# Six shared PSUM banks in an attention-then-Mamba kernel: gates into the convolutions' banks, reciprocals turned in the denominators' bank, and attention steps at fixed half slots

## The chip, the core and the metric

The kernel runs on one core of a Trainium2 chip. The metric is the device time of one execution in microseconds (us). Five engines work side by side: TensorE (PE; its weight loads are shown as PEld), VectorE (DVE), ScalarE (ACT), GpSimd (POOL), and SyncE (SP), which only issues DMA transfers here. Each engine takes its own instructions in the order in which the program put them.

## The reference, cut to what matters

```python
# x: (8, 512, 48, 48) float32; L = 48*48 = 2304 tokens
# layer 0: x = x + attention(group_norm(x)), 8 heads of 64, causal linear attention
Q = elu(q) + 1;  K = elu(k) + 1
den = 1 / (Q . cumsum(K) + 1e-10)
out = (causal sum of K V^T, applied to Q) * den
# layer 1: x = x + mamba_stack(group_norm(x)); 4 blocks of 128 channels, one after the other
xz = u @ Wi.T;  xp, z = split(xz)
xs = silu(causal_conv4(xp) + bc)                    # 256 inner channels
dt, Bm, Cm = split(xs @ Wx.T);  delta = softplus(dt @ Wdt.T + bdt)
h_t = exp(delta A) h_(t-1) + delta xs Bm            # 16 states per channel
y = (sum over states of h C + xs D) * silu(z);  xm = y @ Wo.T
feat = sigmoid(mean x_i) x_i + sigmoid(mean max(x_i, xm)) max(x_i, xm)   # passed to the next block
```

## The kernel before, in words

**Mamba: jobs and slots.** Two streams handle the even and the odd samples. Each of the 8 x 4 blocks (sample, channel block) is cut into six pieces of 384 tokens (`LC`), so there are 192 **jobs**. A job has 8 **slots**; a slot is four scans on VectorE (`Job.scan`, L830, 128 x 385), one product ahead of them (`product`, L809) and a weighing on GpSimd (`weigh`, L846). 1,536 slots follow one another. The decay of every scan, exp(delta A), is computed by ScalarE (`decay`, L819) into a PSUM bank; the k-th decay belongs to the k-th scan, and the bank is free again once that scan has read it. `ahead(n)` issues decays until n are waiting, as long as a bank is spare: three are asked for after each scan, five ahead of the two groups that change ScalarE's table of functions, which are the Silu group (L670 to L675) and the Softplus group (L705).

**Banks.** Six PSUM banks (`BANKS`) are shared by the decays and by everything else that TensorE writes, except the sum over states, which has its own (`yp`, L853). `take` gives out the first spare bank; banks that are freed `late`, that is after a Silu or Softplus group, are kept back for decays where another is spare.

**Halves.** Each slot has two **halves**: one ahead of its four scans, one after the second of them. In a half, `beside` lets the tasks step that are due and for which enough banks are spare; a task is a Python generator whose `yield` says when it may go on (a number of halves after its last step, or a fixed half) and how many banks it needs. So the Python decides the order, and each engine then works its own queue.

**A job's preparation** (`prepare`) runs about ten slots ahead of its scans: two convolutions with the input projection folded in (`conv`, L635, four accumulating matmuls each), two gate projections (`gate`, L646), the Silu group (`xs` twice, `sz` twice), the projection to dt, B, C (L681, copied out at L686), the step projection (L694), Softplus, then writes to DRAM and the repeated reads of `dr`, `dxr`, B and C. A job that is done ends in `finale`: the output projection (L871) one half after the last product with the gate (`gated`, L865), and the maximum on VectorE (`fg`, L882) one half later.

**Attention: chunks.** 192 **chunks** (sample, head pair o, 384 tokens) run beside the jobs, most of them 16 halves apart (`PERIOD`), in step with the jobs. A chunk's steps stand at fixed halves after its start, `at(j)`: projections q, k, v (L288), feature maps (exp and relu on ScalarE at L300 and L301, then L345 for q and L353 for k on VectorE), key sums (L364, L374), turned k and v (L381), denominators and state increments (L393, L398; read at L401 to L410), the reciprocals copied wide (L414) and turned (L418), q times the reciprocals (L423), scores (L431, L436), outputs (L445, L449, L452). A group norm ahead of either layer needs the statistics of a sample (`statistics`, L242) or of one block (`group_norm` at L457).

With the two period lengths equal, a chunk starts at half 3 of a job's 16 halves, and a job's preparation falls on fixed halves as well.

Of the kernel before, what the change touches and what calls it, by code (L numbers as in the profile page):

```python
# [9 lines left out]
F32 = mybir.dt.float32  # L10
# [6 lines left out]
P = 128  # L17
T = 128
LC = 384
# [30 lines left out]
def attention_then_mamba_kernel(  # L50
# [108 lines left out]
            _, o, i = stores.pop(0)  # L159
            nc.sync.dma_start(out=o, in_=i)  # L160

    def group_norm(stats, n, name, bufs):


        bank = Banks()
        yield "1", 1
        mv = small.tile([P, n, 2], F32, tag=f"mv{n}", name=f"mv_{name}", bufs=1)
        for ct in range(n):
            nc.vector.bn_aggr(mv[:, ct, :], stats[:, ct].rearrange("p c s -> p (c s)"))
        mean_ps = bank()  # L170
        nc.tensor.matmul(mean_ps[:, 0:n], grp, mv[:, :, 0], start=True, stop=True)
        yield "1", 0
        gm = small.tile([P, 3, n], F32, tag=f"gm{n}", name=f"gm_{name}", bufs=1)
        nc.vector.tensor_copy(gm[:, 0, :], mean_ps[:, 0:n])
        nc.vector.tensor_sub(gm[:, 1, :], mv[:, :, 0], mean_ps[:, 0:n])
        bank.free()
        if n == 1:
            nc.vector.tensor_scalar(
                gm[:, 2, :], gm[:, 1, :], gm[:, 1, :], mv[:, 0, 1:2], ALU.mult, ALU.add
            )  # L180
        else:
            nc.vector.tensor_mul(gm[:, 2, :], gm[:, 1, :], gm[:, 1, :])
            nc.vector.tensor_add(gm[:, 2, :], gm[:, 2, :], mv[:, :, 1])
        yield "0", 1
        var_ps = bank()
        nc.tensor.matmul(var_ps[:, 0:n], grp, gm[:, 2, :], start=True, stop=True)
        yield "1", 0
        nc.vector.tensor_scalar_add(gm[:, 2, :], var_ps[:, 0:n], 1e-5)
        bank.free()
        norm = small.tile([P, 3, n], F32, tag=f"norm{n}", name=f"norm_{name}", bufs=bufs)  # L190
        nc.gpsimd.tensor_tensor(norm[:, 0, :], gm[:, 2, :], power[:, 0:n], ALU.pow)
        yield "1", 0
        for i, factor in ((0, -1.0), (1, float(L))):
            for ct in range(n):
                nc.vector.tensor_scalar(
                    norm[:, 1 + i, ct : ct + 1],
                    gm[:, i, ct : ct + 1],
                    norm[:, 0, ct : ct + 1],
                    factor,
                    ALU.mult,  # L200
                    ALU.mult,
                )
        return norm
# [5 lines left out]
    def statistics(b):  # L209

        xv = x[b].rearrange("(t p) l -> p t l", p=P)
        stats = small.tile([P, 4, NC, 6], F32, tag="stats_a", name=f"stats_a{b}", bufs=1)
        if b == 0:

            xs = []

            def load(c):
                t = mpool.tile([P, 4, 1 + LC], F32, tag="u", name=f"xs_{c}", bufs=5)[:, :, 0:LC]
                nc.sync.dma_start(out=t, in_=xv[:, :, c * LC : (c + 1) * LC])
                xs.append(t)  # L220

            for c in range(5):
                load(c)
            load_projections(0)
            for c in range(NC):
                for ct in range(4):
                    nc.vector.bn_stats(stats[:, ct, c, :], xs[c][:, ct, :])
                if c == 0:
                    load(5)
                    fetch(0)  # L230
            for o in range(1, 4):
                load_projections(o)
        else:
            for ct in range(4):
                for c in range(NC):
                    yield "2", 0
                    if (ct, c) == (0, 0):
                        nxt = piece(b, 0)
                    xs = nxt
                    i = ct * NC + c + 1  # L240
                    nxt = piece(b, i) if i < 4 * NC else None
                    nc.vector.bn_stats(stats[:, ct, c, :], xs)  # L242
        norms[b] = yield from group_norm(stats, 4, f"a{b}", 2)

    def piece(b, i):
        ct, c = i // NC, i % NC
        xs = apool.tile([P, LC], F32, tag="xs", name=f"xs_{b}_{i}", bufs=2)
        nc.sync.dma_start(out=xs, in_=x[b][ct * P : (ct + 1) * P, c * LC : (c + 1) * LC])
        return xs
# [18 lines left out]
    def chunk(m):  # L268
# [71 lines left out]
        qp, qb = project(0)  # L340
        yield at(1), 0
        ex = feature(qp, qb)
        yield at(2), 0
        q = new("q", 2)
        nc.vector.scalar_tensor_tensor(q, ex, 1.0, qp, ALU.min, ALU.add)  # L345
        bank.free()
        yield at(2, 0), 1
        kp, kb = project(1)
        yield at(3), 0
        ex = feature(kp, kb)  # L350
        yield at(4), 0
        k = new("k", 2)
        nc.vector.scalar_tensor_tensor(k, ex, 1.0, kp, ALU.min, ALU.add)  # L353
        bank.free()
        yield at(4, 0), 1
# [10 lines left out]
            nc.tensor.matmul(kc, ident, before, start=False, stop=True)  # L366
        yield at(8), 0
        if ksum is not None:
            kept = new("kept")
# [16 lines left out]
        nc.scalar.copy(v, turned[1])  # L386
        bank.free(2)

        yield at(12), 1
        both = bank()  # L390
        den = both[:, 0 : 2 * NT]
        for i in range(NT):
# [3 lines left out]
        for i in range(more):  # L396
            for h in heads_of:
                nc.tensor.matmul(ds[h, i, :], kl[:, i, h], v[:, i, h], start=True, stop=True)  # L398
        yield at(14), 0
        rd = small.tile([P, 2 * NT], F32, tag="rd", name=f"rd_{n}", bufs=1)  # L400
        nc.vector.tensor_scalar_add(rd, den, 1e-10)  # L401
        nc.vector.reciprocal(rd, rd)
# [3 lines left out]
        for i in range(more):  # L406
            if c == 0 and i == 0:
                nc.vector.tensor_copy(S[:, place[1], :], ds[:, 0, :])
            else:
                nc.vector.tensor_add(S[:, place[i + 1], :], S[:, place[i], :], ds[:, i, :])  # L410
        bank.free()
        yield at(15), 0
        rdb = new("rdb", 1, (P, 2 * NT, 64))
        nc.scalar.copy(rdb, rd.unsqueeze(2).to_broadcast([P, 2 * NT, 64]))  # L414
        yield at(16), 1
        rb = bank()[:, 0:LC].rearrange("p (i t) -> p i t", i=NT)
        for i in range(NT):
            nc.tensor.transpose(  # L418
                rb[:, i, :], rdb[:, 2 * i : 2 * i + 2, :].rearrange("p e d -> p (e d)"), ident
            )  # L420
        yield at(18), 0

        nc.vector.tensor_mul(q, q, rb.rearrange("p i t -> p (i t)"))  # L423
        bank.free()
# [29 lines left out]
        nc.vector.bn_stats(stats[:, 0, c, :], xr)  # L454
        save(x1s[b][tile_rows, cols], xr)
        if c + 1 == NC:
            norm = yield from group_norm(stats, 1, f"m{b}_{o}", 8)  # L457
            flush()
            done[b, o] = norm

# [155 lines left out]
    class Job:  # L616
# [6 lines left out]
        def prepare(self):  # L623
# [17 lines left out]
                    )  # L641
                return xc

            def gate(h):
                zp = bank()[:, 0:LC]
                nc.tensor.matmul(  # L646
                    zp,
                    wi[:, 256 + h * P : 256 + (h + 1) * P],
                    xi[:, c0 + 3 : c0 + 3 + LC],
                    start=True,  # L650
                    stop=True,
                )
                return zp


            while converting or not st.scaled:
                yield "1w", 0
            converting.append(n)
            yield "1", 1
            xc0 = conv(0)  # L660
            yield "2", 2
            xc1 = conv(1)
            zp0 = gate(0)
            yield "1", 0
# [5 lines left out]
            nc.scalar.activation(xs[:, 0, :], xc0, AF.Silu, bias=pv[:, 0:1])  # L670
            bank.free()
            zp1 = gate(1)
            nc.scalar.activation(xs[:, 1, :], xc1, AF.Silu, bias=pv[:, 1:2])
            nc.scalar.activation(sz[0], zp0, AF.Silu)
            nc.scalar.activation(sz[1], zp1, AF.Silu)  # L675
            converting.clear()
            bank.free(3, late=True)
            yield "1", 1
            dps = bank()
            for h in range(2):  # L680
# [54 lines left out]
            def rows(m, q):  # L735
# [5 lines left out]
                    )  # L741
                (self.B, self.C)[m][q] = t

            for h in range(2):
                yield "1", 0
                nc.gpsimd.tensor_tensor(delta[:, h, :], delta[:, h, :], xs[:, h, :], ALU.mult)  # L746
            first = 2 * self.start
            yield "2", 0
            xsrc = spread("xscr")
            spreading.clear()  # L750
# [206 lines left out]
    def finale(job):  # L957
# [4 lines left out]
        if job.c == NC - 1:  # L962
            yield from job.stream.pass_on()

    begun, put, counted = 0, 0, list(range(1, B))

    def begin(latest):

        nonlocal begun, put
        while counted and times[parts.index((counted[0], 0, 0))] - 64 <= half_no[0]:  # L970
# [53 lines left out]
    def at(k):  # L1024
        return jobs[k // SLOTS], k % SLOTS
# [166 lines left out]
```

## Time and profile before

| | before |
|---|---|
| median of 3 runs | 9331.63 us (9327.02 to 9333.99) |
| profiled execution | 9323.3 us, span 9321.5 us |
| busy: VectorE | 8348.4 us (90% of the span) |
| busy: GpSimd | 8080.8 us (87%) |
| busy: TensorE | 7735.1 us (83%) |
| busy: ScalarE | 6580.2 us (71%) |
| moved by DMA | 1642.84 MB, mean 176 GB/s |
| first 100 us: VectorE, GpSimd busy | 42.10 us, 20.79 us |

How to read what follows: a row of a timeline is start (us), duration (us), engine, line and operation, then out<-in with its sizes and how many instructions were merged. Brackets at its end give how long the engine had stood idle before it and what ended that. A row of the waits is: engine, line and tile that waited, `<-` whom it waited for, total us, times, longest us. One job takes about 48 us (9321.5 / 192 = 48.5).

### The profile page before, as it was taken

What the parts mean: (1) busy time and instruction counts of PE and PEld (TensorE: products, weight loads), DVE (VectorE), ACT (ScalarE), POOL (GpSimd) and SP (SyncE); (2) the same over time, 40 slices, a digit from 0 to 9 for tenths busy, and PEclk for the clock granted to TensorE, in tenths of its full rate; (3) what the DMA queues carried; (4) which work ended last, traced back from release to release, by engine and by line L of the source; (5) the groups of instructions that cost most, each with busy time, mean ns of one, the idle gap of its engine ahead of it and who ended that gap; (6) DMA issues with size and microseconds to landing.
All of it is one profiled execution on the core that took longest, in us unless ns stands there. A gap on an engine that the chain in (4) does not pass through costs nothing.

```text
span 9321.5 us, 120629 instructions
## 1 busy us (share of the span) xinstructions
PE 7735.1 (83%) x35714; PEld 3673.0 (39%) x35714; DVE 8348.4 (90%) x11640; ACT 6580.2 (71%) x12656; POOL 8080.8 (87%) x5635
## 2 busy tenths in 40 slices
PE   7888888888888888888888888888888888888865
PEld 4444444433344444443343444443333434444321
DVE  3899999999999999999999999999999999999997
ACT  3677777777777777777777777776777777777775
POOL 2788888889988898889998888888998888888998
PEclk9999999999999999999999999999999999999977
DMA  6566666667666666666766666667666666666654
GB/s 189 158 169 173 175 174 168 180 189 198 188 169 176 177 179 172 176 183 189 196 182 178 174 175 173 174 170 194 192 184 182 176 176 172 173 171 175 167 153 129
DMA packets 1002899, 1642.84 MB, mean 176 GB/s; under 512 B 138592, under 2 KB 797312, under 8 KB 1002240
## 3 DMA queue, kind: packets, MB, share of 16 engines
q1 hardware_dynamic: 1002240, 1635.13, 64.1%
q8 instruction: 283, 4.64, 0.2%
q14 instruction: 376, 3.08, 0.1%
HBM read 1309.06 MB, written 325.58 MB: 175 GB/s over the span
## 4 chain that ended last, share of the span: by engine, by line
DVE 39%; ACT 20%; PE 18%; issue 7%; DMA 7%; POOL 6%; SPq 2%; DVEq 0%; POOLq 0%; ACTq 0%
DVE u L830 23%; DVE u L809 8%; PE bank L288 7%; ACT bank L819 6%; PE bank L635 4%; POOL u L846 4%; ACT L819 3%; PE yp L853 3%; PE bank L646 2%; ACT L705 2%; DMA B<-scr 2%; DMA C<-scr 1%; ACT bank L301 1%; ACT delta L705 1%; DVE sm L436 1%
## 5 line engine op out<-in xcount | busy, mean ns | idle before, releaser
L830 DVE TENSOR_TENSOR_SCAN u<-bank,u 128x385 f32<-128x385 f32 (+1 forms) x6144 | 5475.1, 938 | 530.5 <-ACT bank L819 503.2
L846 POOL TENSOR_TENSOR u<-u,C 128x1536 f32<-128x1536 f32 x1536 | 4885.1, 3180 | 219.5 <-DVE u L830 112.6
L819 ACT ACTIVATE bank<-dr,av 128x385 f32<-128x385 f32 (+1 forms) x6144 | 3431.3, 579 | 1556.9 <-DVE u L830 1113.3
L853 PE MATMUL yp<-u,cst 128*64 128x384 f32 x12288 | 2429.9, 514 | 282.7 <-ACT yp L787 146.3
L798 POOL TENSOR_TENSOR u<-B,dxr 128x512 f32<-128x512 f32 x1536 | 1959.9, 1276 | 22.4 <-DMA dxr<-xscr 19.0
L288 PE MATMUL bank<-xn,wq_sb 128*128 128x384 f32 x4608 | 1855.1, 552 | 48.8 <-DVE u L830 31.7
L809 DVE TENSOR_TENSOR u<-B,dxp 128x1024 f32<-128x1024 f32 x1536 | 1834.7, 1195 | 10.7 <-ACT dxp L782 10.7
L853 PEld LDWEIGHTS yp<-u,cst 128*64 128x64 f32 x12288 | 788.3, 139 | 1476.6 <-issue 903.5
L635 PE MATMUL bank<-xi,wk 128*128 128x384 f32 x3072 | 1118.2, 507 | 280.1 <-ACT kl L385 172.7
L288 PEld LDWEIGHTS bank<-xn,wq_sb 128*128 128x128 f32 x4608 | 929.1, 212 | 862.9 <-issue 215.1
L635 PEld LDWEIGHTS bank<-xi,wk 128*128 128x128 f32 x3072 | 563.7, 193 | 862.2 <-ACT kl L385 254.1
L844 POOL COPY state<-u 128x4 f32<-128x4 f32 x1280 | 243.8, 190 | 740.6 <-DVE u L830 738.0
L300 ACT ACTIVATE ex<-bank,bqkv_sb 128x384 f32<-128x384 f32 x384 | 221.3, 576 | 561.6 <-PE bank L288 539.2
L787 ACT ACTIVATE yp<-xs,pv 128x384 f32<-128x384 f32 x384 | 223.4, 582 | 405.7 <-DVE yz L865 405.7
L819 ACT ACT_TABLE_LOAD x382 | 490.1, 1283 | 6.7
L746 POOL TENSOR_TENSOR delta<-delta,xs 128x384 f32<-128x384 f32 x384 | 385.8, 1005 | 95.5 <-DMA dscr<-delta 84.3
L418 PE MATMUL bank<-cst,rdb 128*128 128x128 f32 x576 | 112.7, 310 | 426.1 <-DVE u L830 334.7
L694 PE MATMUL bank<-dbc,wd 9*128 9x384 f32 x768 | 316.3, 524 | 65.1 <-ACT dbc L686 29.0
L646 PE MATMUL bank<-xi,wi 128*128 128x384 f32 x768 | 297.8, 500 | 59.8 <-ACT xs L670 59.8
L871 PE MATMUL bank<-yz,wo 128*128 128x384 f32 x768 | 297.6, 509 | 34.1 <-DVE yz L865 19.4
L449 PE MATMUL bank<-sm,v 128*64 128x128 f32 x2304 | 257.2, 301 | 42.4 <-DVE u L830 40.6
L418 PEld LDWEIGHTS bank<-cst,rdb 128*128 128x128 f32 x576 | 66.8, 153 | 558.9 <-ACT xb L601 272.5
(109 smaller groups left out, 7860.3 us busy)
## 6 DMA issues: line engine op xcount, KB each, us to landing
B<-scr SPq DMA_DIRECT2D x1536, 192.0 KB
C<-scr SPq DMA_DIRECT2D x1536, 192.0 KB
xn<-xn SPq DMA_DIRECT2D x192, 768.0 KB
dr<-dscr SPq DMA_DIRECT2D x768, 192.0 KB
dxr<-xscr SPq DMA_DIRECT2D x768, 192.0 KB
dscr<-delta SPq DMA_DIRECT2D x192, 384.0 KB
xscr<-delta SPq DMA_DIRECT2D x192, 384.0 KB
xn<-in_x SPq DMA_DIRECT2D x48, 768.0 KB
```

The lines of the kernel that those rows point to most:

```text
L288: nc.tensor.matmul(ps, wq_sb[:, kt, j * 512 + o * P : j * 512 + (o + 1) * P], xn[:, kt, :], start=(kt == 0), stop=(kt == 3),)
L635: nc.tensor.matmul(xc, wk[:, k, h * P : (h + 1) * P], xi[:, c0 + k : c0 + k + LC], start=(k == 0), stop=(k == 3),)
L646: nc.tensor.matmul(zp, wi[:, 256 + h * P : 256 + (h + 1) * P], xi[:, c0 + 3 : c0 + 3 + LC], start=True, stop=True,)
L694: nc.tensor.matmul(vp, wd[32:41, h * P : (h + 1) * P], dbc[32:41, :], start=True, stop=True)
L746: nc.gpsimd.tensor_tensor(delta[:, h, :], delta[:, h, :], xs[:, h, :], ALU.mult)
L798: nc.gpsimd.tensor_tensor(u[:, :, :, 1 + LC - TAIL :], self.B[s % 4][:, :, cols].unsqueeze(2).to_broadcast(shape), self.dxr[s // 4][:, :, ...
L809: nc.vector.tensor_mul(u[:, :, :, 1 : 1 + LC - TAIL], self.B[s % 4][:, :, cols].unsqueeze(2).to_broadcast(shape), self.dxp.unsqueeze(1).to ...
L819: nc.scalar.activation(dA[:, cols], self.dr[h][:, g, cols], AF.Exp, scale=self.w[6][:, 2 * h + g, q + j : q + j + 1],)
L830: nc.vector.tensor_tensor_scan(u[:, j, g, cols], dA[:, cols], u[:, j, g, cols], 0.0, ALU.mult, ALU.add,)
L846: nc.gpsimd.tensor_tensor(h, h, self.C[s % 4].unsqueeze(2).to_broadcast([P, NG, 2, LC]), ALU.mult)
L853: nc.tensor.matmul(self.yp[g * 64 : g * 64 + 64, 0:LC], pair_sum, u[:, j, g, 1:], start=False, stop=(s % 4 == 3 and j == NG - 1), skip_gro ...
L871: nc.tensor.matmul(self.xm[:, 0:LC], self.w[2][:, h, :], self.yz[:, h, :], start=(h == 0), stop=(h == 1),)
```

## The change

1. **Gates.** `gate` gets a bank passed in. Each gate projection is written into the bank of the convolution that has just been read by Silu, so the Silu group uses two banks instead of three or four. The convolutions, the second of which needed two spare banks, and the group now stand at fixed halves (20, 18 and 17 halves ahead of the job's first scan) instead of at the earliest half that fits.
2. **Reciprocals.** The chunk's bank of denominators and state increments (`both`) isn't freed after L410; the reciprocals are turned into that bank. Denominators start at `at(11)` (were 12), their reading at 13 (14), the wide copy at 14 (15), the turning at 15 (16), q times the reciprocals at 16 (18).
3. **q and k.** k's projection comes at `at(2)` ahead of q's step on VectorE (L345), which goes to `at(3)`; before, q's step came first and its bank was freed.
4. **Statistics.** A later sample's 24 `bn_stats` come one per 16 halves (two halves after their load) instead of one every two halves; the group norm of a block stands at fixed halves.
5. **Small things.** Both products delta*xs stand in one half; `kept` uses the buffer tag `before`; `stats_a` has two buffers.

The diff, cut:

```diff
-    def group_norm(stats, n, name, bufs):
+    def group_norm(stats, n, name, bufs, places=("1", "1", "0", "1", "1")):
...
-            for ct in range(4):
-                for c in range(NC):
-                    yield "2", 0
-                    if (ct, c) == (0, 0):
-                        nxt = piece(b, 0)
-                    xs = nxt
-                    i = ct * NC + c + 1
-                    nxt = piece(b, i) if i < 4 * NC else None
-                    nc.vector.bn_stats(stats[:, ct, c, :], xs)
+            when = begins[b] + b % 2
+            for i in range(4 * NC):
+                yield (when - 2, 1) if b > 1 else "1", 0
+                xs = piece(b, i)
+                yield (when, 1) if b > 1 else "1", 0
+                nc.vector.bn_stats(stats[:, i // NC, i % NC, :], xs)
+                when += PERIOD
...
-        yield at(2), 0
-        q = new("q", 2)
+        yield at(2), 1
+        kp, kb = project(1)
+        yield at(3), 0
+        q, k = new("q", 2), new("k", 2)
         nc.vector.scalar_tensor_tensor(q, ex, 1.0, qp, ALU.min, ALU.add)
         bank.free()
-        yield at(2, 0), 1
-        kp, kb = project(1)
-        yield at(3), 0
         ex = feature(kp, kb)
...
-        yield at(12), 1
+        yield at(11), 1
         both = bank()
...
-        yield at(14), 0
+        yield at(13), 0
         rd = small.tile([P, 2 * NT], F32, tag="rd", name=f"rd_{n}", bufs=1)
...
-        bank.free()
-        yield at(15), 0
+        yield at(14), 0
         rdb = new("rdb", 1, (P, 2 * NT, 64))
         nc.scalar.copy(rdb, rd.unsqueeze(2).to_broadcast([P, 2 * NT, 64]))
-        yield at(16), 1
-        rb = bank()[:, 0:LC].rearrange("p (i t) -> p i t", i=NT)
+        yield at(15), 0
+
+        rb = both[:, 0:LC].rearrange("p (i t) -> p i t", i=NT)
...
-        yield at(18), 0
+        yield at(16), 0
         nc.vector.tensor_mul(q, q, rb.rearrange("p i t -> p (i t)"))
         bank.free()
...
-            norm = yield from group_norm(stats, 1, f"m{b}_{o}", 8)
+            norm = yield from group_norm(
+                stats, 1, f"m{b}_{o}", 8, [(times[m] + j, 1) for j in (26, 27, 29, 30, 31)]
+            )
...
-            yield "1", 1
+            first = 2 * self.start
+            yield (first - 20, 1), 1
             xc0 = conv(0)
-            yield "2", 2
+            yield (first - 18, 2), 1
             xc1 = conv(1)
-            zp0 = gate(0)
-            yield "1", 0
+            yield (first - 17, 1), 0
...
             nc.scalar.activation(xs[:, 0, :], xc0, AF.Silu, bias=pv[:, 0:1])
-            bank.free()
-            zp1 = gate(1)
+
+            gate(0, xc0)
             nc.scalar.activation(xs[:, 1, :], xc1, AF.Silu, bias=pv[:, 1:2])
-            nc.scalar.activation(sz[0], zp0, AF.Silu)
-            nc.scalar.activation(sz[1], zp1, AF.Silu)
+            gate(1, xc1)
+            nc.scalar.activation(sz[0], xc0, AF.Silu)
+            nc.scalar.activation(sz[1], xc1, AF.Silu)
             converting.clear()
-            bank.free(3, late=True)
+            bank.free(2, late=True)
```

More of the change, by code (lines that the diff above doesn't have):

```diff
@@ L160, in flush @@
             nc.sync.dma_start(out=o, in_=i)
-    def group_norm(stats, n, name, bufs):
+    def group_norm(stats, n, name, bufs, places=("1", "1", "0", "1", "1")):
         bank = Banks()
-        yield "1", 1
+        yield places[0], 1
         mv = small.tile([P, n, 2], F32, tag=f"mv{n}", name=f"mv_{name}", bufs=1)
@@ L171, in group_norm @@
         nc.tensor.matmul(mean_ps[:, 0:n], grp, mv[:, :, 0], start=True, stop=True)
-        yield "1", 0
+        yield places[1], 0
         gm = small.tile([P, 3, n], F32, tag=f"gm{n}", name=f"gm_{name}", bufs=1)
@@ L183, in group_norm @@
             nc.vector.tensor_add(gm[:, 2, :], gm[:, 2, :], mv[:, :, 1])
-        yield "0", 1
+        yield places[2], 1
         var_ps = bank()
         nc.tensor.matmul(var_ps[:, 0:n], grp, gm[:, 2, :], start=True, stop=True)
-        yield "1", 0
+        yield places[3], 0
         nc.vector.tensor_scalar_add(gm[:, 2, :], var_ps[:, 0:n], 1e-5)
@@ L191, in group_norm @@
         nc.gpsimd.tensor_tensor(norm[:, 0, :], gm[:, 2, :], power[:, 0:n], ALU.pow)
-        yield "1", 0
+        yield places[4], 0
         for i, factor in ((0, -1.0), (1, float(L))):
@@ L211, in statistics @@
         xv = x[b].rearrange("(t p) l -> p t l", p=P)
-        stats = small.tile([P, 4, NC, 6], F32, tag="stats_a", name=f"stats_a{b}", bufs=1)
+        stats = small.tile([P, 4, NC, 6], F32, tag="stats_a", name=f"stats_a{b}", bufs=2)
         if b == 0:
@@ L342, in chunk @@
         ex = feature(qp, qb)
-        yield at(2), 0
-        q = new("q", 2)
+        yield at(2), 1
+        kp, kb = project(1)
+        yield at(3), 0
+        q, k = new("q", 2), new("k", 2)
         nc.vector.scalar_tensor_tensor(q, ex, 1.0, qp, ALU.min, ALU.add)
         bank.free()
-        yield at(2, 0), 1
-        kp, kb = project(1)
-        yield at(3), 0
         ex = feature(kp, kb)
         yield at(4), 0
-        k = new("k", 2)
         nc.vector.scalar_tensor_tensor(k, ex, 1.0, kp, ALU.min, ALU.add)
@@ L368, in chunk @@
         if ksum is not None:
-            kept = new("kept")
+            kept = new("before")
             nc.scalar.copy(kept[64:128], kc[64:128])
@@ L642, in conv, with gate @@
                 return xc
-            def gate(h):
-                zp = bank()[:, 0:LC]
+            def gate(h, zp):
                 nc.tensor.matmul(
@@ L652, in gate @@
                 )
-                return zp
             while converting or not st.scaled:
@@ L658, in prepare @@
             converting.append(n)
-            yield "1", 1
+            first = 2 * self.start
+            yield (first - 20, 1), 1
             xc0 = conv(0)
-            yield "2", 2
+            yield (first - 18, 2), 1
             xc1 = conv(1)
-            zp0 = gate(0)
-            yield "1", 0
+            yield (first - 17, 1), 0
             xs = self.xs = mpool.tile([P, 2, LC], F32, tag="xs", name=f"xs_{n}")
@@ L742, in rows @@
                 (self.B, self.C)[m][q] = t
+            yield "1", 0
             for h in range(2):
-                yield "1", 0
                 nc.gpsimd.tensor_tensor(delta[:, h, :], delta[:, h, :], xs[:, h, :], ALU.mult)
-            first = 2 * self.start
             yield "2", 0
@@ L965, in attention_then_mamba_kernel @@
     begun, put, counted = 0, 0, list(range(1, B))
+    begins = {}
+    for b in counted:
+        first = times[parts.index((b, 0, 0))]
+        begins[b] = (first - 20) // PERIOD * PERIOD - 4 * NC * PERIOD - 1 if b > 1 else first - 64
     def begin(latest):
         nonlocal begun, put
-        while counted and times[parts.index((counted[0], 0, 0))] - 64 <= half_no[0]:
+        while counted and begins[counted[0]] - 4 <= half_no[0]:
             tasks.append(Task(statistics(counted.pop(0))))
```

## The prediction, written before the changed kernel ran

> **What bounds the kernel now.** I read the page's busy shares first, then VectorE's waits away from start and end (300 to 9000 us), then timelines of single jobs on all engines. No engine is full:
>
> ```profile
> PE 7735.1 (83%) x35714; PEld 3673.0 (39%) x35714; DVE 8348.4 (90%) x11640; ACT 6580.2 (71%) x12656; POOL 8080.8 (87%) x5635
> ```
>
> VectorE is nearest, and no row of its waits names GpSimd as a partner of weight, so the span is VectorE's work plus VectorE's gaps:
>
> ```profile
> DVE u L830 <- ACT bank L819: 473.9, 184, 4.6
> DVE q L345 <- ACT bank L301: 105.5, 53, 4.2
> DVE k L353 <- ACT bank L301: 55.6, 134, 1.0
> DVE gm_m L188 <- PE bank L186: 29.4, 31, 1.1
> ```
>
> With some 45 us of small rows that is 710 us, or 3.9 us in each of the 180 jobs of this window. The first row is one gap per job, at the Silu group. ScalarE's timeline and VectorE's there:
>
> ```profile
> 5012.16 1.28 ACT L670 ACT_TABLE_LOAD   x1
> 5013.46 0.58 ACT L670 ACTIVATE xs<-bank,pv 128x384 f32<-128x384 f32 x1
> 5015.05 0.49 ACT L675 ACTIVATE sz<-bank 128x384 f32<-128x384 f32 x1 [0.15 <-PE bank L646]
> 5015.56 1.28 ACT L819 ACT_TABLE_LOAD   x1
> ...
> 5017.47 0.96 DVE L830 TENSOR_TENSOR_SCAN u<-bank,u 128x384 f32<-128x384 f32 x1 [3.17 <-ACT bank L819]
> ```
>
> From the last decay ahead of the group (ends 5012.14) to the next one's end ScalarE needs 5.3 us; the scans that were supplied run out 3.17 us before that. The second row is rarer and is the one that decides my forecast. Here is such a case, on VectorE, ScalarE and TensorE:
>
> ```profile
> 4361.72 0.53 DVE L423 TENSOR_TENSOR q<-q,bank 128x384 f32<-128x384 f32 x1
> 4365.23 0.55 DVE L345 SCALAR_TENSOR_TENSOR q<-ex,bank 128x384 f32<-128x384 f32 x1 [2.98 <-ACT bank L301]
> ...
> 4357.44 1.28 ACT L705 ACT_TABLE_LOAD   x1
> 4358.74 0.87 ACT L705 ACTIVATE delta<-bank 128x384 f32<-128x384 f32 x2
> 4364.17 0.58 ACT L300 ACTIVATE ex<-bank,bqkv_sb 128x384 f32<-128x384 f32 x1 [2.66 <-PE bank L288]
> ...
> 4359.28 0.55 PE L418 MATMUL bank<-cst,rdb 128*128 128x128 f32 x3 [2.38 <-ACT delta L705]
> 4359.66 4.47 PE L288 MATMUL bank<-xn,wq_sb 128*128 128x384 f32 x8
> 4363.93 1.56 PE L871 MATMUL bank<-yz,wo 128*128 128x384 f32 x4
> ```
>
> TensorE stands until Softplus has read its bank, then needs 4.47 us for a q projection that takes 2.85 us where it comes straight after other matmuls (the row at 5034.81), and only then does the output projection, whose result `fg` (L882) needs.
>
> **What the Trainium skill says.** "TensorE: Matmul & The Clock Gate", Part 1: after an idle stretch the array runs at half clock until it has been busy for some 3.4 us. The trace agrees in kind: pairs of matmuls 0.64 us apart after the 2.4 us stop, 0.36 us apart otherwise. "ScalarE: Activation LUTs", What ACT_TABLE_LOAD costs: 1283 ns for the load plus about 1380 ns of drain; the trace has the 1283 ns, and nothing like the drain (Silu starts 0.02 us after). "Perfetto Trace Analysis", Sequencer Loop: an instruction in an engine's queue waits there for its semaphore. So what stands behind it waits too, as L871 above.
>
> **The change part by part.** Work is the same in count on every engine, so only gaps can move. I use the built order of each queue, old and new, with durations from the trace.
>
> *Silu group.* The last decay ahead of it is now that of the next slot's first scan, and it takes the bank that slot 7's second scan frees; call that scan's end t = 0. ScalarE: wait 0.24, decay 0.59, state copy to 0.95, load to 2.24, `xs` ends 2.82. The first gate may start only now. Before, one gate of two was in this position: `xs` ended 5014.04, its `sz` started 5015.05, 1.01 us later. So `sz` starts at 3.83; the second gate follows 0.72 later (four matmuls 1.50), `sz` from 4.55 to 5.04, load to 6.33, decay to 6.94. VectorE: two scans 1.72, product 1.11, the reading of denominators and states (L401 to L410, 0.89, moved here), one scan 0.86: 4.58. Gap 2.36; the moved `bn_stats` (0.48, 144 of them) bring the mean to 2.0, against 473.9/184 = 2.58 now: **-110 us**. Behind the waiting gates in TensorE's queue stand L681 (1.45) and the gather of slot 6 (1.51); they end about 7.3, and the next item, L418, can't start before its wide copy is done at 9.1: 1.8 us to spare. If TensorE cools there, the gates cost up to 0.6 more, and this gain is gone.
>
> *Softplus and the q projection.* Now that `both` is kept to the end of the reciprocals, no decay's bank is spare when q starts: in the built order 176 of 192 q projections wait for a Softplus bank, where 31 did, and in 175 jobs the output projection follows right behind. Count from the scan after the Silu gap, R = 0. VectorE reaches `fg` after 3 scans 2.58, product 1.11, 2 scans 1.72, L423 0.53, 2 scans 1.72, product 1.11, L865 0.47, 2 scans 1.72: R + 11.0. Softplus comes behind the decay that waits for L423 (R + 5.9): its load starts at R + 6.9, its first half has read its bank at R + 8.7. Then q, after some 2.5 us without work, 4.4, and L871, 1.4: R + 14.5. **A new gap of 3.5 us at `fg`** in 175 jobs: +612 us. Before, the same `fg` came at R + 12.3, with L423 and L345 ahead of it and q started at R + 6.4 (from 5020.31 on), just in time. With q at 2.85 us the gap is 1.9.
>
> *q and k.* L345 now stands two scans behind `fg`, so its wait goes: -105 us. L353 still stands two scans on; k's projection follows the gather that waits for ScalarE's L787 behind q's exp and relu. By the same count 0.5 us in 179 chunks against 55.6 us now: +35 us. Bounds: no wait, or 1.0 us each (+120).
>
> *Reciprocals into `both`.* Taking no bank removes TensorE's wait at L418 for a scan's bank (`PE bank L418 <- DVE u L830`, 334.7 us of its idle time), which no VectorE row shows as its own; L418 is done at about R + 3, needed at R + 5.4: hidden by scans. *Group norms at fixed halves* remove L188's wait: -29 us. *Statistics:* the same loads, one per 16 halves, on SP two halves ahead; SP passes the B and C reads there, and its own waits on those are 210 us over 247 cases, below 1 us each against some 6 us of lead: 0, at worst 1 us x 144. *Both delta products together, `kept` in `before`* (the next load of it comes 8 halves on): 0; GpSimd's slack of 13% and SP's lead cover them, at worst +50 us. *Start* (first 300 us): 0; TensorE is busy 93.83 of the second 100 us. Bounds -20 to +40.
>
> Sum: -110 + 612 - 105 + 35 - 29 = +403 us. I take off 25 us for jobs in which other delays already fall into the gap at `fg`. Against the profiled execution's own 9323.3 us that is 9701; the median of the runs lies 8 us higher: **9710 us**.
>
> **The rivals.** A difference under 0.2% (19 us) can't be told from no change here.
>
> *Faster: the Softplus wait is absorbed.* If TensorE isn't idle long enough to slow down, and Softplus comes 2 us earlier than I count, `fg` waits at most as long as L345 did. Then -110 - 105 - 29, and up to 40 us more at k: 9050 to 9310, say 9090. For it speaks that ScalarE waited 539 us for projections (row L300) without VectorE losing more than 105. Against it: the 31 old cases with this order, such as the one above. The point from which it decides is 1.4 us of mean gap at `fg`: 1.4 x 175 = 245 us, all of the gains.
>
> *In between: a warm TensorE.* q at 2.85 us, gap 1.9: +333 - 209 = +124 us, about 9450.
>
> *Worse: both stalls cold.* Gates slow as well (+0.6 us x 184 = +110) and a gap at `fg` of 4.2 us, as where ScalarE has an xb to scale (L601, 0.69 us) ahead of Softplus: +735 in place of 612. Together 9940.
>
> That the change doesn't do what it says is excluded by the built order.
>
> **How the numbers follow.** Forecast 0.56, warm 0.14, worst 0.10, faster 0.17, and 0.03 that gains and gap cancel. The likeliest case alone spans 9560 to 9850. For 8 in 10, I add the warm case and the upper edge of the rivals: 9300 to 9880; most of the faster case and half of the worst are left out. Faster by over 0.2%: 0.17; within: 0.04; slower: 0.79.
>
> **What would show it.** Right: among VectorE's waits a new row `fg <- PE` of the output projection's line near 500 to 650 us with some 175 cases; TensorE waiting for `delta` of Softplus 175 times ahead of a q projection of over 4 us; ScalarE's wait at ex near 2 us per chunk; the L830 row down to some 370 us; rows for L345 and L188 gone. Wrong: no `fg` row over 200 us, or a Silu row as large as now.

## The result, and the profile after

| | before | after |
|---|---|---|
| median of 4 runs | 9332.6 us (9327.0 to 9334.0) | 9635.8 us (9633.9 to 9642.8) |
| ratio to before, 95% interval | | **1.0327 [1.031, 1.0345]** |
| span of the profiled execution | 9321.5 us | 9641.0 us |
| VectorE: span less busy time | 973 us | 1279 us |
| TensorE's mean granted clock, 300 to 9000 us | 0.96 | 0.91 |

The change makes the kernel 3.3% slower. Line numbers now are those of the changed kernel: scans L826, decays L815, q, k and v projections L286, Softplus L702, output projection L867, `fg` L878. The engines' line of the page:

```profile
PE 8065.2 (84%) x35714; PEld 3875.1 (40%) x35714; DVE 8362.3 (87%) x11640; ACT 6596.9 (68%) x12657; POOL 8082.5 (84%) x5635
```

VectorE has the work it had (8348.4 us before), so all but 14 of the 319.5 us of longer span are gaps. TensorE's instruction count is the same too, yet it was busy for 330 us more: the same matmuls ran slower. VectorE's waits, 300 to 9300 us, and after them the row of the kernel before that the second one replaces:

```profile
DVE fg L878 <- PE bank L867: 633.7, 175, 4.8
DVE u L826 <- ACT bank L815: 345.7, 187, 8.3
DVE k L349 <- ACT bank L299: 35.5, 109, 1.4
...
DVE gm_m L188 <- PE bank L186: 1.7, 2, 1.4
```

```profile
DVE u L830 <- ACT bank L819: 496.4, 192, 4.7
```

The first row is new. The second, the gap at the Silu group, was 496.4 us over 192 cases in the same window before (2.58 us each, now 1.85). L345's row for q is gone, k's went from 55.6 to 35.5, L188's from 29.4 to 1.7. These five changes are +633.7 - 150.7 - 105.5 - 20.1 - 27.7 = +329.7 us, against +319.5 in the span. (The window leaves out the last 341 us of the changed kernel and 21 us of the one before; over whole runs the Silu row goes from 503.2 to 364.1 us, by 139 instead of 151.) Who makes TensorE late is in the groups of the page (busy time, mean ns of one, then the idle time before them and what ended it):

```profile
L286 PE MATMUL bank<-xn,wq_sb 128*128 128x384 f32 x4608 | 1965.6, 579 | 351.3 <-ACT delta L702 347.8
```

The projections stood 348 us waiting for Softplus's reading. One such place, on TensorE and on VectorE:

```profile
5047.71 2.83 PE L849 MATMUL yp<-u,cst 128*64 128x384 f32 x8
5051.90 5.24 PE L286 MATMUL bank<-xn,wq_sb 128*128 128x384 f32 x8 [1.36 <-ACT delta L702]
5056.97 1.45 PE L867 MATMUL bank<-yz,wo 128*128 128x384 f32 x4
```

```profile
5052.01 0.56 DVE L861 TENSOR_TENSOR yz<-yp,sz 128x384 f32<-128x384 f32 x1
5052.48 1.80 DVE L826 TENSOR_TENSOR_SCAN u<-bank,u 128x385 f32<-128x385 f32 x2
5058.46 0.56 DVE L878 SCALAR_TENSOR_TENSOR fg<-bank,xi 128x384 f32<-128x384 f32 x1 [4.18 <-PE bank L867]
```

The operand `yz` of the output projection was ready at 5052.57 (5052.01 + 0.56), but q's projection was ahead of it in TensorE's queue; it began only when Softplus had read its bank, took 5.24 us, and VectorE stood 4.18 us.

### The profile page after: what moved, and what is told of

The parts are those of the page before. It is cut to its first block, busy times and chain, and to the rows that moved or that the text cites. A ratio compares the mean times of both kernels' runs of the same rounds, so it can differ in the third digit from the quotient of the medians.

```text
span 9641.0 us, 120563 instructions
## 1 busy us (share of the span) xinstructions
PE 8065.2 (84%) x35714; PEld 3875.1 (40%) x35714; DVE 8362.3 (87%) x11640; ACT 6596.9 (68%) x12657; POOL 8082.5 (84%) x5635
## 4 chain that ended last, share of the span: by engine, by line
DVE 41%; PE 26%; ACT 18%; issue 8%; POOL 4%; DMA 2%; SPq 1%; POOLq 0%; DVEq 0%; ACTq 0%
DVE u L826 26%; PE bank L286 12%; DVE u L805 9%; ACT bank L815 6%; PE bank L633 5%; PE yp L849 4%; PE bank L643 3%; POOL u L842 3%; ACT L815 2%; ACT L702 2%; ACT L666 2%; ACT bank L299 1%; DVE sm L432 1%; DVE k L349 1%; ACT sz L672 1%
## 5 line engine op out<-in xcount | busy, mean ns | idle before, releaser
L826 DVE TENSOR_TENSOR_SCAN u<-bank,u 128x385 f32<-128x385 f32 (+1 forms) x6144 | 5483.8, 942 | 364.7 <-ACT bank L815 364.1
L815 ACT ACTIVATE bank<-dr,av 128x385 f32<-128x385 f32 (+1 forms) x6144 | 3421.8, 580 | 1265.1 <-DVE u L826 1092.1
L849 PE MATMUL yp<-u,cst 128*64 128x384 f32 x12288 | 2601.9, 531 | 195.5 <-ACT yp L783 106.2
L286 PE MATMUL bank<-xn,wq_sb 128*128 128x384 f32 x4608 | 1965.6, 579 | 351.3 <-ACT delta L702 347.8
L633 PE MATMUL bank<-xi,wk 128*128 128x384 f32 x3072 | 1259.1, 559 | 428.4 <-DVE u L826 375.7
L286 PEld LDWEIGHTS bank<-xn,wq_sb 128*128 128x128 f32 x4608 | 977.7, 223 | 1370.2 <-ACT delta L702 540.9
L849 PEld LDWEIGHTS yp<-u,cst 128*64 128x64 f32 x12288 | 846.5, 142 | 1386.0 <-issue 947.1
L633 PEld LDWEIGHTS bank<-xi,wk 128*128 128x128 f32 x3072 | 623.2, 213 | 1039.0 <-DVE u L826 547.9
L298 ACT ACTIVATE ex<-bank,bqkv_sb 128x384 f32<-128x384 f32 x384 | 222.9, 580 | 856.5 <-PE bank L286 856.5
L878 DVE SCALAR_TENSOR_TENSOR fg<-bank,xi 128x384 f32<-128x384 f32 x192 | 106.9, 557 | 635.3 <-PE bank L867 635.3
L691 PE MATMUL bank<-dbc,wd 9*128 9x384 f32 x768 | 349.6, 580 | 11.9 <-ACT dbc L683 9.1
L414 PE MATMUL bank<-cst,rdb 128*128 128x128 f32 x576 | 104.6, 291 | 303.2 <-ACT rdb L409 301.6
L867 PE MATMUL bank<-yz,wo 128*128 128x384 f32 x768 | 312.0, 530 | 12.5 <-DVE yz L861 8.2
L678 PE MATMUL bank<-xs,wx 128*40 128x384 f32 x768 | 286.8, 496 | 1.1 <-DVE q L419 1.1
```

What stands on the lines that cost most here:

```text
L286: nc.tensor.matmul(ps, wq_sb[:, kt, j * 512 + o * P : j * 512 + (o + 1) * P], xn[:, kt, :], start=(kt == 0), stop=(kt == 3),)
L633: nc.tensor.matmul(xc, wk[:, k, h * P : (h + 1) * P], xi[:, c0 + k : c0 + k + LC], start=(k == 0), stop=(k == 3),)
L691: nc.tensor.matmul(vp, wd[32:41, h * P : (h + 1) * P], dbc[32:41, :], start=True, stop=True)
L815: nc.scalar.activation(dA[:, cols], self.dr[h][:, g, cols], AF.Exp, scale=self.w[6][:, 2 * h + g, q + j : q + j + 1],)
L826: nc.vector.tensor_tensor_scan(u[:, j, g, cols], dA[:, cols], u[:, j, g, cols], 0.0, ALU.mult, ALU.add,)
L849: nc.tensor.matmul(self.yp[g * 64 : g * 64 + 64, 0:LC], pair_sum, u[:, j, g, 1:], start=False, stop=(s % 4 == 3 and j == NG - 1), skip_gro ...
```

## The experiments

Each ratio is against runs of the kernel before on the same chip. Waits are VectorE's, 300 to 9300 us, in us; "scans" is the row of the scans for a decay. "q behind Softplus" counts, in the built order (the order in which the Python puts the instructions into each engine's queue), the q projections that wait for a bank that Softplus reads, directly or through the turning of the reciprocals just ahead of them. A dash is no row of weight. The statistics, the group norms and the small things of the change were not run by themselves.

| kernel | us | ratio [95%] | q behind Softplus | `fg` | scans | k | rd |
|---|---|---|---|---|---|---|---|
| after | 9635.8 | 1.0327 [1.031, 1.0345] | 176 | 634 | 346 | 36 | - |
| no extra decays | 9336.6 | 1.0012 [1.0004, 1.0021] | 0 | 75 | 426 | 191 | - |
| old reciprocals | 9568.6 | 1.0262 [1.0246, 1.0277] | 179 | 650 | 21 | 38 | 142 |
| preparation a half earlier | 9486.5 | 1.0169 [1.0152, 1.0186] | 32 | 108 | 369 | 79 | 173 |
| whole old preparation | 9560.5 | 1.0248 [1.0233, 1.0263] | 34 | 111 | 659 | 70 | 51 |
| before with the new preparation | 9492.0 | 1.0174 [1.0158, 1.0189] | 179 | - | 55 | 71 | 213 |
| TensorE kept busy ahead of q | 9498.3 | 1.0185 [1.017, 1.02] | 176 | 288 | 346 | 42 | - |
| old gates | 9632.6 | 1.0321 [1.0304, 1.0338] | 177 | 625 | 40 | 34 | 317 |
| k ahead alone | 9567.6 | 1.0262 [1.0245, 1.0279] | 177 | 600 | 350 | 4 | - |
| **k ahead, no extra decays** | **9165.3** | **0.983 [0.9816, 0.9845]** | 0 | 104 | 415 | 4 | - |
| before, no extra decays | 9464.1 | 1.0152 [1.0137, 1.0168] | 30 | - | 768 | 47 | - |

### 1. Is Softplus's bank the cause? No extra decays ahead of it

```diff
             delta = mpool.tile([P, 2, LC], F32, tag="delta", ...)
-            ahead(DEPTH + 2)
+            ahead(DEPTH)
```

Two decays fewer ahead of Softplus leave a bank spare, and q takes the one that q times the reciprocals (L419) frees.

> The changed kernel with one token altered: ahead(DEPTH) in place of ahead(DEPTH + 2) in front of Softplus, so that the bank of the reciprocals, free in that half, goes to the q projection and not to a further decay. In the built order 175 q projections then wait for L419 (q times reciprocals) on VectorE and none for Softplus. Theory (the wait for a Softplus bank holds q, behind it the output projection, and so fg): the fg row falls from 634 us to under 80, the row of scans waiting for decays grows by some 60 to 100 us because Softplus has one decay less ahead of it, k may wait 50 us more: 9100 to 9200 us. Rival A (TensorE is slower everywhere, mean granted clock 0.90 against 0.95, and fg only shows it): at most 300 us come back, 9340 or more. Rival B (the gates in the convolutions' banks cost it): not touched here, 9550 or more.

VectorE's waits:

```profile
DVE u L826 <- ACT bank L815: 425.6, 423, 7.3
DVE k L349 <- ACT bank L299: 190.6, 168, 3.5
DVE fg L878 <- PE bank L867: 74.6, 48, 1.7
```

The time falls by (1.0327 - 1.0012), some 294 us, and 559 us of `fg`'s row go: without the wait for that bank there is no stop of weight. But 80 us of it come back at the scans, as expected, and 155 at k, where 50 were expected. The time therefore lies 137 us above the expected range, close to the 9340 of rival A (a TensorE that is slower everywhere). The row of `fg` speaks against rival A, and experiment 7 settles it. k's projection now stood behind a gather of u (L849) whose product on GpSimd wasn't done:

```profile
5043.18 1.51 PE L849 MATMUL yp<-u,cst 128*64 128x384 f32 x8 [2.79 <-POOL u L794]
5044.62 2.85 PE L286 MATMUL bank<-xn,wq_sb 128*128 128x384 f32 x8
```

### 2. Does keeping `both` cause it? The old reciprocals

The changed kernel, with the denominators at half 12 again, their bank freed after reading, and the reciprocals turned into a bank of their own:

```diff
-        yield at(11), 1
+        yield at(12), 1
...
+        bank.free()
...
-        rb = both[:, 0:LC].rearrange("p (i t) -> p i t", i=NT)
+        yield at(16), 1
+        rb = bank()[:, 0:LC].rearrange("p (i t) -> p i t", i=NT)
```

> The changed kernel with the reciprocals as before: own bank, old halves (12, 14, 15, 16, 18), the denominators' bank freed after L410. The prediction put the Softplus wait down to that bank being kept. If that is so, q finds another bank and the time falls below 9350 us. In the built order, though, 179 q projections still wait for Softplus, since both stand in half 3 of a job now: then the fg row stays, smaller by about 1 us each because L423 is ahead of fg again (some 400 to 500 us), while the Silu gap grows by the 0.9 us of L401 to L410 that are behind it again (+165 us): 9520 to 9680 us.

VectorE's waits, then TensorE's:

```profile
DVE fg L878 <- PE bank L867: 650.0, 179, 5.3
```

```profile
PE bank L414 <- ACT delta L702: 465.9, 158, 4.0
```

`fg` waits as before the edit. Now it is mostly the turning, just ahead of q in TensorE's queue, that takes Softplus's bank. **Keeping `both` is not what makes the stop**, though the prediction gave it as the reason. The edit still gains 61 us: the scans' row goes from 346 to 21, and waits of 142 us at the denominators and 61 more at the group norm (L188) appear. The time is in the expected range, but by luck: `fg`'s row was to fall to 400 to 500 us and the Silu gap to grow by 165. All told the reciprocals' new place, with the denominators one half earlier, costs a little, where the prediction had put zero.

### 3. Do coinciding halves cause it? The preparation one half earlier

```diff
-            yield (first - 20, 1), 1
+            yield (first - 21, 1), 1
...
-            yield (first - 18, 2), 1
+            yield (first - 19, 2), 1
...
-            yield (first - 17, 1), 0
+            yield (first - 18, 1), 0
```

> The changed kernel with the convolutions and the Silu group one half earlier (21, 19 and 18 halves ahead instead of 20, 18 and 17); the reciprocals stay in the denominators' bank. Softplus then comes a half ahead of the q projection; in the built order 145 q projections wait for a scan and 32 for Softplus. Theory (coinciding halves make the wait): the fg row falls to 100 to 200 us, the Silu gap is some 0.5 to 1 us longer (+90 to +180 us): 9200 to 9380 us. If keeping the denominators' bank is what costs, nothing is won: 9600 or more.

```profile
DVE rd L397 <- PE bank L394: 173.0, 155, 2.8
DVE fg L878 <- PE bank L867: 108.0, 32, 4.8
```

With Softplus one half earlier 32 q projections are left behind it, and `fg` waits in just 32 cases. So it is the half in which the new preparation puts Softplus that makes q take its bank. The time is above what was expected, in the main since the Silu group now meets the denominators (L397, 173 us, none before the edit); k's row and one at a group norm (L174) grow by 44 and 51 us. A further kernel was to ask for those denominators one half earlier:

```diff
-        yield at(11), 1
+        yield at(10), 1
```

> As the run with the preparation one half earlier (9487 us), and the denominators one half earlier too (halves 10 instead of 11), so that in TensorE's queue they stand ahead of the gates that wait for Silu. If the 173 us at L397 are that queueing, they go: the row falls below 30 us and the time to 9290 to 9340 us, about the kernel before. If the freed time only moves into the Silu gap behind it, the scans' row grows from 368 to 500 us or more and the time stays above 9430.

TensorE's order is the same but for 4 of its 35714 matmuls, and the row did not move (173.9 us); it is a repeat of the one above: 9498.1 us, 1.0173 [1.0156, 1.019]. Whether an earlier place would help stays open.

### 4. The preparation by itself, both ways

First, the changed kernel with the whole old preparation: earliest halves in place of fixed ones, gates in own banks, the products delta*xs in two halves.

```diff
-            yield (first - 20, 1), 1
+            yield "1", 1
             xc0 = conv(0)
-            yield (first - 18, 2), 1
+            yield "2", 2
             xc1 = conv(1)
-            yield (first - 17, 1), 0
+            zp0 = gate(0)
+            yield "1", 0
```

> The changed kernel with the whole job preparation as before: gates in banks of their own, convolutions and Silu group at the earliest half that fits, the two delta products in two halves. Everything else of the change stays (reciprocals in the denominators' bank, q and k, statistics, group norms, kept). In the built order 144 q projections wait for a scan and 34 for Softplus. Theory (the preparation's new halves bring Softplus into the half of the q projection): fg waits near 100 us, not 634; the other rows as in the run with the preparation one half earlier (scans about 370 to 470, denominators about 170): 9400 to 9520 us. Rival (the denominators' bank kept longer is the cause): fg stays above 400 us and the time above 9560.

```profile
DVE u L828 <- ACT bank L817: 658.7, 304, 8.1
DVE fg L880 <- PE bank L869: 110.5, 41, 4.9
```

`fg` behaves as expected; the scans' row is almost twice what it was, so the time is longer than expected (it is the rival's time, but not the rival's row). A variant with the denominators at half 10 had the same waits within 6 us:

> The changed kernel with the preparation as before and the denominators one half earlier: a candidate to beat both kernels. If the waits at the denominators go and fg waits for Softplus in 34 jobs only: 9230 to 9350 us. If the Silu gap takes what the denominators give: 9400 to 9480.

It took 9554.4 us, 1.024 [1.0224, 1.0255], outside both expected ranges; TensorE's order is that of the run above, so it tells nothing new.

Second, the kernel before with nothing but the new preparation (the same diff the other way round; line numbers of that kernel, q at L345, denominators at L401):

> The kernel before with the job preparation of the changed kernel alone (gates into the convolutions' banks, fixed halves, both delta products in one half). In the built order 179 q projections wait for Softplus. Theory (preparation's halves): an fg or q row near 600 us and a time of 9540 to 9680 us. Rival (the denominators' bank): fg small, 9200 to 9350 us, since the Silu group then has more decays ahead of it.

```profile
DVE q L345 <- ACT bank L301: 412.7, 150, 4.2
DVE rd L401 <- PE bank L398: 212.6, 150, 2.8
```

**The new preparation alone brings the stop into the kernel before.** 179 q projections are behind Softplus where 31 were. VectorE meets it at q's step because in that kernel q's step stands ahead of `fg` in its queue; that moving q's step to `at(3)` hands the wait on to `fg` is read from the order, and no run moves that step alone. The time is 48 us below the expected range. In time the preparation is also not all of it: alone it costs 165 of the 303 us, and taking it out of the changed kernel gains only some 74, because the scans' row then grows by 313.

### 5. How much of it is a cold TensorE? Matmuls ahead of q

"Cold" means that TensorE runs slowly, at a granted clock of 0.50, as it did from 5047.7 to 5050.5 us in the place shown above. Ten matmuls with zero weights, into columns of `yp` that nobody reads, fill the stop ahead of every q projection from chunk 17 on.

```diff
+        if m >= 16:
+            for _ in range(FILL):
+                nc.tensor.matmul(yp[:, LC : LC + T], zero, cst[:, 0:T], start=False, stop=True, ...)
```

> The changed kernel with ten extra matmuls with a zero weight, 128 columns each, ahead of every q projection from the 17th chunk on (into unused columns of yp's bank, read by nobody). They fill the stop in which TensorE waits for Softplus. If the slow q projection after the stop (about 4.4 us against 2.85) is a part of the fg gap, as the prediction has it, the q projection's pairs come 0.36 us apart and fg waits some 1.5 us less: 9350 to 9450 us. If TensorE's clock has no part in it: within 30 us of 9636, or more where the ten matmuls (about 2.2 us) take longer than the stop.

TensorE (`L343` are the fillers; the trace shows each of the ten as two instructions), then VectorE's waits (L891 is `fg`, L874 `yz`):

```profile
5017.32 2.50 PE L343 MATMUL yp<-cst,zero 128*128 128x128 f32 x20
5020.42 2.85 PE L289 MATMUL bank<-xn,wq_sb 128*128 128x384 f32 x8 [0.60 <-ACT delta L715]
```

```profile
DVE fg L891 <- PE bank L880: 288.4, 176, 3.4
DVE yz L874 <- PE yp L343: 179.7, 126, 5.8
```

q still starts only after Softplus, but takes 2.85 us here; over the whole trace 175 of these 176 q projections take under 3.5 us, where 144 of 176 took over 4 us in the changed kernel. The mean gap at `fg` falls from 633.7 / 175 = 3.62 to 288.4 / 176 = 1.64 us: as an estimate from these rows, 345 us of `fg`'s row came of q's lower pace and 288 the wait for Softplus itself. It is an estimate because the fillers also make q start later and VectorE reach `fg` later, which pull the gap opposite ways. The time gains less (some 133 us) and stays above the expected range, because the fillers write into the tile whose sums `yz` reads, which then waits 180 us.

### 6. The gates: a bank of their own again

```diff
-            def gate(h, zp):
+            def gate(h):
+                zp = bank()[:, 0:LC]
...
+            zp0 = gate(0)
             nc.scalar.activation(xs[:, 0, :], xc0, AF.Silu, bias=pv[:, 0:1])
...
+            zp1 = gate(1)
```

> The changed kernel with each gate projection in a bank of its own again (the fixed halves, the reciprocals and all else as changed). My theory: the gates are not what makes `fg` wait, so that row stays at 600 to 700 us; ScalarE's wait for the gate's bank (106 us in all) falls under 40, and of that some 60 to 100 us come off the scans' row (346 us): 9540 to 9600 us. Rival: with two more banks held through the Silu group the decays get fewer, so the scans' row grows instead and the time is 9640 us or longer.

VectorE's waits, without the row of `fg` (625.1 us):

```profile
DVE rd L397 <- PE bank L394: 316.7, 179, 2.8
DVE u L827 <- ACT bank L816: 40.4, 9, 8.3
```

ScalarE's wait for the gates is nearly gone (138 us for both, now 10), the scans' row fell by 305 us, and against the 9540 to 9600 us that were expected no time was won. The second gate now stands ahead of the state increments (L394) in TensorE's queue and waits there for the first `xs`; VectorE, which needs those for rd, stands as long as it stood for the decay. The gap at the Silu group changed its name, not its size.

### 7. A version that beats both kernels

Experiment 1 left k's wait. k's projection one half earlier, alone and with the first edit:

```diff
-        yield at(2), 1
+        yield at(1, 0), 1
         kp, kb = project(1)
```

> The changed kernel with k's projection at half 4 (`at(1, 0)`) alone; `ahead(DEPTH + 2)` ahead of Softplus stays. My theory: q's projection still waits for Softplus's bank 177 times, so `fg`'s row stays at 580 to 700 us; k's row (36 us) goes to under 20; 9600 to 9650 us. Rival (what counts is k's place in TensorE's queue, not Softplus's bank): the row of `fg` falls under 300 us and the time under 9400.

> As in the first experiment, `ahead(DEPTH)` in place of `ahead(DEPTH + 2)` before Softplus, and k's projection one half earlier (half 4, `at(1, 0)`), so that it stands ahead of the gather of u in TensorE's queue. My theory (Softplus's bank and TensorE's order set the stops): the stop at `fg` stays gone (its row under 100 us) and k's row of VectorE's waits falls from 190 us to under 60; the scans' row stays near 420: about 9130 to 9200 us, the fastest of all. Rival (the banks are what is short: a projection that takes its bank one half earlier takes it from a decay): k's row falls but the scans' row grows by as much or more, above 550 us, and the time is 9330 us or longer.

Alone, k's row goes (36 to 4 us) and `fg` stays at 600 us: 9567.6 us. That is 33 us below the expected range, as `fg`'s row lost 34 us that I had not counted on. With both edits, VectorE's waits and one stretch of TensorE:

```profile
DVE u L826 <- ACT bank L815: 415.0, 392, 7.5
DVE fg L878 <- PE bank L867: 103.7, 68, 1.7
...
DVE k L349 <- ACT bank L299: 4.4, 3, 1.5
```

```profile
5030.19 3.07 PE L286 MATMUL bank<-xn,wq_sb 128*128 128x384 f32 x8
5033.09 1.45 PE L867 MATMUL bank<-yz,wo 128*128 128x384 f32 x4
5034.38 2.74 PE L286 MATMUL bank<-xn,wq_sb 128*128 128x384 f32 x8
```

q starts right behind its predecessor, the output projection follows, and `fg` ran at 5034.59 with no wait. **9165.3 us, 0.983 [0.9816, 0.9845] of the kernel before**, the fastest of all. Against experiment 1 the scans' row did not grow (426 to 415), so the rival (banks are what is short) falls. So does rival A of experiment 1: TensorE's mean granted clock is 0.932 in this profile and 0.948 in that of the kernel before, and yet this kernel is the faster one. The edits gain some 294 and 60 us alone, and 464 together: the first creates k's wait, the second takes it away.

Is this owed to `ahead(DEPTH)` in any order of the work? The control is that edit in the kernel before:

> The kernel before, with `ahead(DEPTH)` in place of `ahead(DEPTH + 2)` ahead of Softplus: is what the last experiments gained owed to that edit alone? My theory says no: in the kernel before only 31 of 192 q projections wait for Softplus's bank, and this edit leaves 30 of them, so it takes nothing away: 9310 to 9350 us. Rival (two decays fewer ahead of Softplus free a bank and a place on ScalarE in any order of the work): the row of q's waits (105 us) halves and the time falls under 9290 us. If the decays are missed instead, the scans' row grows from 474 us to over 550 and the time passes 9380.

```profile
DVE u L830 <- ACT bank L819: 768.1, 347, 4.5
...
DVE q L345 <- ACT bank L301: 15.6, 29, 1.9
```

There it costs 1.5%, where 9310 to 9350 us were expected. q's wait falls by 90 us as the rival had it, but the scans run out of decays for 272 us more, the third case named. So the 1.7% need the two edits together, and the first of them pays in the changed order only; k's edit was not tried in the kernel before. Why the same two decays are missed for 272 us in one order and for 80 in the other was not tried.

## Why the prediction was right or wrong

**The stop at `fg`: right in kind and size.** 3.5 us in 175 jobs, 612 us, was forecast; 3.62 us in 175 jobs, 633.7 us, was measured, with the predicted chain (Softplus's bank, q's projection, output projection, `fg`). 144 of 176 such q projections took over 4 us. Experiments 1 and 3 take the wait away from two sides, and the row falls to 75 and 108 us. One sign named can't be judged: ScalarE's wait at `ex` is 856.5 us in 378 cases, 2.3 us each but 4.5 us per chunk.

**The reason given for it: wrong.** "Now that `both` is kept to the end of the reciprocals, no decay's bank is spare when q starts" fails in experiment 2, where `both` is freed and the stop stays. It is the preparation's fixed halves (experiments 3 and 4) that put Softplus next to q in nearly every job, together with the two decays asked for ahead of it (experiment 1). The built order showed that q waits and for whom, and the forecast number rests on that; the step from there to why was argued only.

**Cold TensorE: right in size, not in what makes it cold.** The forecast gave a gap of 1.9 us with q at 2.85 us; experiment 5 has 1.64. But the prediction put q's lower pace down to the stop for Softplus itself ("after some 2.5 us without work"). In 118 of 176 cases the clock records of the changed kernel show the half clock since before that stop began (last section).

**Silu group: right in sign, a little small.** A mean gap of 2.0 was forecast for 2.58, and 1.85 measured: the row fell by 150.7 us, not 110. TensorE's cooling there, feared as the end of this gain, didn't show: ScalarE waited 106 us for the first gate over 192 jobs. Experiment 6 adds what the sum did not hold: the old form of the gates gives no worse a time, so the gates' banks are not where this gain comes from.

**q's wait gone: right** (-105). **Group norms: right** (-28 for -29). **k: wrong sign**, +35 forecast and -20 measured: 109 cases of 0.33 us in place of 179 of 0.5. **Reciprocals at no cost: wrong by a little**, undoing them gains 61 us (experiment 2).

**The sum.** 378 us over the profiled execution before were forecast, 319.5 came: k's 55 and Silu's 41 too many, 22 too few at `fg`, 10 more in small rows, less the 25 taken off for overlaps. The rest of the distance between 9710 and 9635.8 us is the step from profile to median: 8 us were added, while the median lies 5 us under the span after. That errors of both signs meet in this sum is luck.

**The rivals.** The absorbed wait needed a mean gap at `fg` under 1.4 us. Not even the warm TensorE of experiment 5 gets there; the wait must be taken out, as in experiments 1 and 7. Both stalls cold did not happen: the first gate cost ScalarE 0.55 us a job.

## What to carry to other kernels

When steps are fixed to slots of equal period, look at which of them now meet in every period: a bank taken over from a neighbour cost no more than 105 us (all waits of q's step together) where it happened in 31 of 192 rounds, and 634 us where it happened in 176. In an in-order queue, ask for each new wait what stands behind it, and price that too at the speed that the engine has in that place of the trace. And an edit that fails alone (k ahead) or in another order (two decays fewer) may be half of the best version: take the largest new row away, read which row grew, and take that away too.

## What was not expected of the hardware

The q projection, eight matmuls of 128x384, takes 2.85 us behind other matmuls and 5.24 us at 5051.90, behind a stop of 1.36 us. The stop is not what slowed it. A job earlier in the same trace a longer one left q at full speed:

```profile
5003.48 2.85 PE L286 MATMUL bank<-xn,wq_sb 128*128 128x384 f32 x8 [1.55 <-ACT delta L702]
```

At 5051.90 TensorE was slow already: the gather ahead of the stop (5047.71) took 2.83 us where it takes 1.51 at other times (experiment 1), at a granted clock of 0.50 (its records have the half clock from 5046.5 to 5056.8). In the 20 us before that gather no stop was over 1.51 us, so the clock was halved without a longer one. Of the 176 q projections with the output projection behind them, 118 had the half clock since before their stop. In experiment 5 none started at half clock. Which of the earlier stops takes the clock down was not tried; one that each job has is the turning's wait for its wide copy (L414 for L409, 302 us over 175 cases). Over the whole run the same 35714 matmuls kept TensorE busy for 7735 us before and 8065 us after.
